# Third mixer: the next sequence's front in 18 pieces and the last sequence's end in 4, each in a slot of its own

## The chip, the cores and the metric

The kernel runs on one core of a Trainium2 chip. The core has a matrix engine (PE, its weight loads shown apart as PEld), a vector engine (DVE), a scalar engine (ACT), a general engine (POOL) and a queue that issues transfers (SP). Each engine works through its own instructions strictly in their order and waits on semaphores for the others. The metric is the device time of one execution in microseconds (us): the median of three runs of the kernel before is 4921.96 us, the runs lie between 4916.99 and 4925.75 us.

## The reference

The model has four layers, each a mixer and a feed-forward part, on 8 sequences of 512 positions by 256 channels in float32. Every part is added to the residual stream X in the same way: `x = x + layernorm(part(layernorm(x)))`. Only the third mixer (called L2 in the code) is touched. Cut to what matters it is causal attention with 16 heads of 16 channels:

```python
q, k, v = silu(x @ Wq.T), silu(x @ Wk.T), silu(x @ Wv.T)   # per head, 16 channels
r_q, r_k = norm(q), norm(k)
scores = (q / (r_q + 1e-6)) @ (k / (r_k + 1e-6)).T * (r_q * q_scale) * (r_k * k_scale)
out = softmax(where(causal, scores, -inf)) @ v
return out @ Wo.T
```

The factor that a head's vector gets, `r / (r + 2e-6 ...)`, needs a square root, which the kernel takes on DVE by a bit trick and three Newton steps (`rsqrt`).

## The kernel before

Everything of a layer for all 8 sequences is written as one Python program. A scheduling layer then orders each engine's queue: instructions that are ready by its own time model go first in the order in which the program wrote them, an instruction whose inputs are late is overtaken, and semaphores are added for every dependence. Buffers come from pools: a pool tile with `bufs=1` cannot be written for the next sequence until its last reader of this sequence is done.

In `l2_attn` (line 1299) the work of one sequence has three parts.

- The **front** (`front`, line 1355, a Python generator; each `yield` ends a piece). `K.late` loads the second layer's feed-forward result (tile `yl`) and adds its normed value to X: `add_norm` takes the statistics of four tiles on DVE (`bn_stats`, `bn_aggr`, then `rsqrt` on 128x4 numbers: tiles `onst`, `onmv`, `onv`, `ony`, `onh`, `onw`, `onb`), scales on ACT (`yn`) and adds on POOL (`X`, two halves). `K.norm` takes the statistics of the new X (`lnst` to `lny`) and writes `xn`, all on DVE. `K.norm_T` turns `xn` on PE (`pxT`) and copies it on ACT (`xT`). Four pieces multiply a block of rows by the weights of q and k (`pqk`), with tanh on ACT (`thqk`), the product on DVE (`qkp`), its square on POOL (`sq`) and the sum over each head on DVE (`ss`). The fifth goes from the sums through `rsqrt` on 128x128 numbers to the factor `f` in one go (tiles `qkny`, `qknh`, `qknw`, `f`), then POOL multiplies `qkp` by `f`; four pieces make v (`pv`, `thv`, `va`).
- The **steps** (the loop at line 1541). Four heads make a quad, a sequence has 4 quads and a quad 4 steps, so a sequence has 16 steps; they are numbered 0 to 15 here. In a step `maxima` makes the scores of four heads for one block of 128 queries (PE: `S`, in two pairs), and DVE takes their masked maxima (`junk`, `mx`). Five steps later `weights` makes the transposed scores (PE: `T`), ACT the exponentials (`PT`) and POOL zeroes the masked corner of the diagonal block; `sums` multiplies by v one step later (PE: `o`). `S` has three PSUM buffers, `T` two: PE can start a score block only when DVE has read the one three before it. `keys` and `strips` turn the next quad's keys and queries (`ptk`, `ptq`) in steps 1 and 2 of a quad; `spread` divides and turns a quad's result back (`pot`, `rs`, `O`).
- The **end** of the last sequence (`finish`, line 1512): it turns O (`pOT`, `OT`), multiplies by Wo (`py`) and calls `add_norm` with the statistics taken straight from PSUM. It is called one step after the last `spread`, in step 8 of the next sequence, as one piece.

A list tells after which steps a piece of the next sequence's front is written; nothing fixes where the scheduling layer then puts it:

```python
PACE = (1, 1, 1, 1, 0, 1, 1, 1, 1, 1, 1, 2, 0, 0, 1, 0)
```

Of the kernel before, what the change touches and what calls it, by code (L numbers as in the profile page):

```python
# [9 lines left out]
F32 = mybir.dt.float32  # L10
I32 = mybir.dt.int32
# [3 lines left out]
ALU = mybir.AluOpType  # L15
# [4 lines left out]
P = 128  # L20
NB = 8
L = 512
NT = 4
D = 256
# [844 lines left out]
def l1_attn(K):  # L869
# [10 lines left out]
    with ExitStack() as es:  # L880
# [12 lines left out]
        nc.gpsimd.tensor_copy(mask[:, L - P:L], K.caus)  # L893
        QT, kT, V, OT = {}, {}, {}, {}
        RATE = (0, 0, 3, 5, 5, 5, 10, 9)
# [55 lines left out]
        def weigh(b, h, PT):  # L951
            po = pO.tile([P, L], F32, tag="o", name=f"o{b}_{h}")
            for kt in range(NT):
                nc.tensor.matmul(
                    po[:, kt * P:L], lhsT=V[b][:, kt, :], rhs=PT[:, kt, kt * P:L],
                    start=(kt == 0), stop=(kt == NT - 1))
            nc.scalar.copy(OT[b][:, h, :], po)

        def finish(b):
            K.project_out(  # L960
                b, [(OT[b][:, h, :], wo[:, h, :]) for h in range(H)], pmm, "mm", s1, leave=True,
                parts=4)

        def behind(b, h, qt, p):

            if qt == 0:
                if h == 0:
                    OT[b] = s1.tile([P, H, L], F32, tag="OT", name=f"OT{b}")
                PT[b, h] = sT.tile([P, NT, L], F32, tag="PT", name=f"PT{b}_{h}")
# [34 lines left out]
class Choice:  # L1004
# [7 lines left out]
    E, NL, K = 48, 10, 128  # L1012
# [286 lines left out]
def l2_attn(K):  # L1299
# [4 lines left out]
    nc, tc = K.nc, K.tc  # L1304
    w = K.W["l2_attn"]
    W = w[:, 0:1536].rearrange("p (k n) -> p k n", k=2)
    row = w[:, 1536:1568]
    wo = w[:, 2048:2560].rearrange("p (k n) -> p k n", k=2)
    with ExitStack() as es:
        def pool(name, bufs, **kw):  # L1310
            return es.enter_context(tc.tile_pool(name="l2" + name, bufs=bufs, **kw))
        cst, sb, s1, s3 = pool("c", 1), pool("a", 2), pool("b", 1), pool("d", 3)
        pmm = pool("pm", 2, space=PSUM)
# [33 lines left out]
        def twice_silu(dst, ps, h, uid):  # L1347

            t = sb.tile([P, 512], F32, tag="th", name="th" + uid)[:, 0:16 * h]
            nc.scalar.activation(t, ps, AF.Tanh, scale=0.5)  # L1350
            return nc.vector.scalar_tensor_tensor(
                dst, t.rearrange("p (h d) -> p h d", h=h), 1.0,
                ps.rearrange("p (h d) -> p h d", h=h), ALU.add, ALU.mult)

        def front(b, res):

            QKP, VA = qkp[b % 2], va[b % 2]
            K.late(b, s1)
            yield
            xn = K.norm(b, s1)  # L1360
            yield
            xT = K.norm_T(b, s1, pmm, "mm", xn=xn)
            yield
            ss = sb.tile([P, NT * 32], F32, tag="ss", name=f"ss{b}")
            for n in range(NT):
                ps = pmm.tile([P, 512], F32, tag="mm", name=f"pqk{b}_{n}")
                for k in range(2):
                    nc.tensor.matmul(
                        ps, lhsT=xT[:, k, n * P:(n + 1) * P], rhs=W[:, k, 0:512],
                        start=(k == 0), stop=(k == 1))  # L1370
                qk = QKP[:, n, :, 0:16]
                twice_silu(qk, ps, 32, f"qk{b}_{n}")
                sq = s1.tile([P, 32, 16], F32, tag="sq", name=f"sq{b}_{n}")
                nc.gpsimd.tensor_tensor(sq, qk, qk, ALU.mult)
                nc.vector.tensor_reduce(ss[:, n * 32:(n + 1) * 32], sq, AX.X, ALU.add)
                yield

            r = K.rsqrt(ss, NT * 32, "qkn", sb)
            nc.vector.tensor_tensor(r, r, ss, ALU.mult)
            f = sb.tile([P, NT, 32], F32, tag="f", name=f"f{b}")  # L1380
            ff = f.rearrange("p n h -> p (n h)")
            nc.vector.tensor_scalar(ff, r, 2e-6, None, ALU.add)
            nc.vector.reciprocal(ff, ff)
            nc.vector.tensor_tensor(ff, ff, r, ALU.mult)
            nc.vector.tensor_tensor(
                f, f, half_row[:, None, :].to_broadcast([P, NT, 32]), ALU.mult)
            yield
            for n in range(NT):
                nc.gpsimd.tensor_tensor(
                    QKP[:, n, :, 0:16], QKP[:, n, :, 0:16],  # L1390
                    f[:, n, :, None].to_broadcast([P, 32, 16]), ALU.mult)
            res.update(QKP=QKP, VA=VA)
            yield
            for n in range(NT):
                pv = pmm.tile([P, D], F32, tag="mm", name=f"pv{b}_{n}")
                for k in range(2):
                    nc.tensor.matmul(
                        pv, lhsT=xT[:, k, n * P:(n + 1) * P], rhs=W[:, k, 512:768],
                        start=(k == 0), stop=(k == 1))
                res["v"] = twice_silu(VA[:, n, :, 0:16], pv, 16, f"v{b}_{n}")  # L1400
                yield
# [10 lines left out]
        def strips(i):  # L1412

            b, g = quads[i]
            ps = turned(res[b]["QKP"], g, f"q{b}_{g}")
            QTs[i] = s3.tile([P, L], F32, tag="QT", name=f"QT{b}_{g}")
            nc.scalar.copy(QTs[i], ps)
# [31 lines left out]
        def lower(i):  # L1449

            b, g = quads[i]
            ps = turned(mx[i % 2], 0, f"m{b}_{g}")
            nc.vector.tensor_tensor(QTs[i], ps, QTs[i], ALU.add)

        def weights(i, kt, js):

            b, g = quads[i]
            KZ, QT = KZs[i], QTs[i]
            n = L - kt * P
            if js[0] == 0:  # L1460
                PTs[i, kt] = s3.tile([P, 4, L], F32, tag="PT", name=f"PT{b}_{g}_{kt}")[:, :, 0:n]
            PT = PTs[i, kt]
            tiles = []
            for j in js:
                ps = pT.tile([P, L], F32, tag="T", name=f"T{b}_{g}_{kt}_{j}")
                half = slice(64 * (j // 2), 64 * (j // 2) + 64)
                nc.tensor.matmul(  # L1467
                    ps[:, 0:n], lhsT=KZ[half, j % 2, kt * P:(kt + 1) * P],
                    rhs=QT[half, kt * P:L], start=True, stop=True)
                tiles.append(ps)  # L1470
            for j, ps in zip(js, tiles):
                nc.scalar.activation(PT[:, j, :], ps[:, 0:n], AF.Exp)  # L1472
            if js[-1] == 3:

                nc.gpsimd.affine_select(  # L1475
                    PT[:, :, 0:P], PT[:, :, 0:P], pattern=[[0, 4], [1, P]],
                    compare_op=ALU.is_ge, fill=0.0, base=0, channel_multiplier=-1)
# [32 lines left out]
                    rs[:, 4 * n:4 * n + 4, :].to_broadcast([P, 4, 16]), ALU.mult)  # L1510

        def finish(b, O):
            OT = s1.tile([P, 2, L], F32, tag="OT", name=f"OT{b}")
            for k in range(2):
                ps = pmm.tile([P, L], F32, tag="mm", name=f"pOT{b}_{k}")
                for n in range(NT):
                    nc.tensor.transpose(
                        ps[:, n * P:(n + 1) * P], O[:, n, k * P:(k + 1) * P], K.ident)
                nc.scalar.copy(OT[:, k, :], ps)
            K.project_out(  # L1520
                b, [(OT[:, k, :], wo[:, k, :]) for k in range(2)], pmm, "mm", s1, leave=True, parts=2)

        res = [{} for _ in range(NB)]
        fronts = [front(b, res[b]) for b in range(NB)]
        quads = [(b, g) for b in range(NB) for g in range(4)]
        QTs, KZs, PTs, pos, OSs, O = {}, {}, {}, {}, {}, {}
        NQ, LAG, KEYS = len(quads), 5, (1, 2, 3, 0)  # L1530
        PACE = (1, 1, 1, 1, 0, 1, 1, 1, 1, 1, 1, 2, 0, 0, 1, 0)

        padding(0)
        for _ in fronts[0]:
# [6 lines left out]
        for s in range(4 * NQ + LAG + 8):  # L1541
            i, qt = s // 4, 3 - s % 4
            k, kt = (s - LAG) // 4, KEYS[(s - LAG) % 4]
            last, lt = (s - LAG - 1) // 4, KEYS[(s - LAG - 1) % 4]
            for js in ((0, 2), (1, 3)):
                if i < NQ:
                    maxima(i, qt, js)
                if js[0] and 0 <= last < NQ:
                    sums(last, lt)
                if 0 <= k < NQ:  # L1550
                    weights(k, kt, js)
            if qt == 0 and i < NQ:
                lower(i)
            if i + 1 < NQ and qt == 2:
                keys(i + 1)
            if i + 1 < NQ and qt == 1:
                strips(i + 1)
            k, r = (s - LAG - 6) // 4, (s - LAG - 6) % 4
            if r == 0 and 0 <= k < NQ:
                b, g = quads[k]  # L1560
                if g == 0:
                    O[b] = s1.tile([P, NT, D], F32, tag="O", name=f"O{b}")
                spread(b, g, OSs.pop(k), O[b])
                QTs.pop(k)
                KZs.pop(k)
            if r == 1 and 0 <= k < NQ and k % 4 == 3:
                finish(k // 4, O.pop(k // 4))
            b = s // 16 + 1
            if b < NB:
                for _ in range(PACE[s % 16]):  # L1570
                    next(fronts[b], None)

# [654 lines left out]
```

## Time and profile before

| what | us |
|---|---|
| median of three runs | 4921.96 |
| profiled execution, its own time | 4924.23 |
| its span, first to last instruction | 4922.5 |
| third mixer, first score block to last transposed score | 2038.0 to 2808.0 |
| sequence 0 of it (first score block to the next sequence's) | 86.9 |
| sequences 1 to 6 | 97.3, 96.5, 96.7, 97.1, 106.0, 96.4 |
| sequence 7, with 6.0 us put for its last step | 78.8 |

In the profile a line such as `L1438 PE MATMUL S<-KZ,QT` names the code line, the engine, the operation and the tiles written and read. A matmul of float32 is two PE instructions. `idle before ... <-X` is time in which the engine had nothing to do, and what ended it. `PEclk` is the share of PE's full clock that was granted in a stretch.

### The profile page before, as it was taken

The page shows a single profiled execution, that of the slowest core. Times are in us where ns is not written, and L with a number is a line of the kernel's source. Part 1 is how long each engine was busy: PE and PEld are TensorE (multiplying, and loading weights), DVE is VectorE, ACT ScalarE, POOL GpSimd, SP SyncE. Part 2 cuts the span into 40 slices and gives each one's busy share as a digit, 9 for nine tenths or more (in the row PEclk, how much of TensorE's full clock was granted, in tenths as well). Part 3 has the DMA queues.
Part 4 walks back from the last instruction along what each step waited for, and adds up shares of the span by engine and source line. Part 5 has one row for each costly group of instructions (what it writes and reads, how often), then busy time and mean ns, then how long its engine had stood idle before and what let it go on. Part 6 is the DMA issues. An engine that isn't in the chain of part 4 may idle for free.

```text
span 4922.5 us, 56985 instructions
## 1 busy us (share of the span) xinstructions
PE 4245.9 (86%) x19078; PEld 2592.8 (53%) x19078; DVE 2890.7 (59%) x8043; ACT 1883.3 (38%) x3801; POOL 1944.0 (39%) x1283
## 2 busy tenths in 40 slices
PE   8745788999988599699999899788888888899997
PEld 3334676555655599355444455333333333478884
DVE  6998746456757411666666433477777777751115
ACT  5410233344344233344443433455555455421112
POOL 0001211444344243333332200398778779613331
PEclk9877798999999799799999999899999999899999
DMA  3289430100000499100000000011111111126763
GB/s 113 79 185 202 127 83 15 43 9 6 6 9 15 125 253 247 29 5 10 5 5 1 22 1 1 28 50 46 41 46 44 43 44 50 64 86 229 232 200 107
DMA packets 401496, 358.04 MB, mean 73 GB/s; under 512 B 209234, under 2 KB 334020, under 8 KB 400692
## 3 DMA queue, kind: packets, MB, share of 16 engines
q1 hardware_dynamic: 373252, 305.75, 21.8%
q0 software_dynamic: 16272, 31.87, 2.4%
q10 hardware_dynamic: 11680, 16.80, 1.1%
q8 instruction: 151, 2.47, 0.2%
q14 instruction: 141, 1.16, 0.1%
HBM read 288.08 MB, written 66.26 MB: 72 GB/s over the span
## 4 chain that ended last, share of the span: by engine, by line
PE 41%; DVE 15%; POOL 4%; ACT 3%; issue 3%; DMA 1%; POOLq 0%; DVEq 0%; SPq 0%; ACTq 0%
DVE h L1777 7%; PE gb L1856 5%; PE S L1438 4%; PE h L1267 4%; PE g L1605 3%; PE T L1467 3%; PE y L1748 3%; PE yb L1870 3%; DVE dB L1723 2%; PE py L193 2%; PE pc L1670 2%; PE y L1278 2%; PE o L1489 2%; POOL h L1780 1%; PE pi L1656 1%
## 5 line engine op out<-in xcount | busy, mean ns | idle before, releaser
L1780 POOL TENSOR_TENSOR h<-h,C 128x1024 f32<-128x1024 f32 x256 | 596.0, 2358 | 177.2 <-DVE h L1777 143.3
L1748 PE MATMUL y<-h,C 128*128 128x512 f32 x1024 | 537.9, 666 | 97.3 <-POOL h L1780 97.3
L1777 DVE TENSOR_TENSOR_SCAN h<-dA,dB 128x512 f32<-128x512 f32 x512 | 588.8, 1202 | 28.5 <-ACT dA L1774 11.7
L1774 ACT ACTIVATE dA<-dl,A 128x512 f32<-128x512 f32 x512 | 352.6, 691 | 411.0 <-DVE h L1777 402.5
L938 POOL TENSOR_SCALAR p<-p,rs 128x128 f32<-128x128 f32 (+3 forms) x256 | 275.9, 1086 | 416.8 <-DVE rs L937 260.2
L1748 PEld LDWEIGHTS y<-h,C 128*128 128x128 f32 x1024 | 204.1, 210 | 408.5 <-issue 224.8
L182 POOL TENSOR_TENSOR X<-X,yn 128x1024 f32<-128x1024 f32 (+2 forms) x104 | 157.0, 1524 | 578.0 <-ACT yn L177 504.9
L1444 DVE CUSTOM_DVE_ANT_0 junk<-S,mask 128x256 f32<-128x256 f32 (+3 forms) x512 | 249.9, 488 | 174.9 <-PE S L1438 139.1
L1438 PE MATMUL S<-KZ,QT 64*128 64x512 f32 (+3 forms) x1024 | 294.2, 473 | 22.2 <-DVE mx L1444 21.3
L1728 POOL TENSOR_TENSOR dB<-du,B 128x2048 f32<-128x2048 f32 x64 | 289.8, 4528 | 0.1
L1472 ACT ACTIVATE PT<-T 128x128 f32<-128x128 f32 (+3 forms) x512 | 199.9, 435 | 224.3 <-PE T L1467 220.8
L1467 PE MATMUL T<-QT,KZ 64*128 64x384 f32 (+3 forms) x1024 | 251.0, 487 | 15.4 <-ACT PT L1472 14.6
L1856 PE MATMUL gb<-xbT,w_b 128*128 128x256 f32 (+1 forms) x1472 | 255.3, 332 | 1.0 <-ACT ts L2060 0.6
L1723 DVE TENSOR_TENSOR dB<-du,pb 128x2048 f32<-128x2048 f32 x64 | 145.4, 2273 | 170.4 <-PE pb L1720 120.7
L1856 PEld LDWEIGHTS gb<-xbT,w_b 128*128 128x128 f32 x1472 | 230.2, 191 | 23.1 <-ACT ts L2060 0.8
L1862 DVE TENSOR_TENSOR hTb<-sb,gb 128x512 f32<-128x512 f32 x71 | 48.8, 687 | 325.4 <-PE gb L1856 314.2
L1475 POOL TENSOR_SCALAR_AFFINE_SELECT PT<-PT 128x512 f32<-128x512 f32 x128 | 81.4, 636 | 330.9 <-ACT PT L1472 330.9
L1438 PEld LDWEIGHTS S<-KZ,QT 64*128 64x128 f32 x1024 | 140.7, 192 | 114.6 <-issue 49.3
L1272 ACT ACTIVATE hT<-h,w_l_ffn 128x128 f32<-128x128 f32 x384 | 109.5, 368 | 198.0 <-PE h L1267 198.0
L1267 PE MATMUL h<-xgT,w 128*128 128x128 f32 x1536 | 185.1, 279 | 0.0
L105 DVE BATCH_NORM_STATS2 lnst<-X 128x6 f32<-128x256 f32 x256 | 99.5, 417 | 135.3 <-POOL X L182 134.4
L1267 PEld LDWEIGHTS h<-xgT,w 128*128 128x128 f32 x1536 | 178.2, 194 | 0.0
(510 smaller groups left out, 9003.9 us busy)
## 6 DMA issues: line engine op xcount, KB each, us to landing
w_b<-l3f_w SPq DMA_DIRECT2D x138, 512.0 KB
w<-l1f_w SPq DMA_DIRECT2D x48, 1024.0 KB
C<-xdd SPq DMA_DIRECT2D x128, 256.0 KB
B<-xdd SPq DMA_DIRECT2D x64, 256.0 KB
w<-l1f_w SPq DMA_DIRECT2D x48, 256.0 KB
toep<-l0fd SPq DMA_DIRECT2D x32, 320.0 KB
X<-x SPq DMA_DIRECT2D x16, 512.0 KB
toep<-l0fd SPq DMA_DIRECT2D x32, 256.0 KB
```

The costliest lines, as they stand in the source:

```text
L938: nc.gpsimd.tensor_scalar(p[:, 0:n], p[:, 0:n], rs, None, ALU.mult)
L1267: nc.tensor.matmul(ph[:, j, :], lhsT=w1[:, s, c, m * P:(m + 1) * P], rhs=xgT[:, c, :], start=(c == 0), stop=(c == 1))
L1438: nc.tensor.matmul(ps[:, 0:n], lhsT=QT[half, qt * P:n], rhs=KZ[half, j % 2, 0:n], start=True, stop=True)
L1444: nc.vector.tensor_tensor_reduce(out=junk[:, 0:n], in0=ps[:, 0:n], in1=mask[:, L - n:L], scale=1.0, scalar=-3.0e38, op0=ALU.add, op1=ALU.m ...
L1467: nc.tensor.matmul(ps[:, 0:n], lhsT=KZ[half, j % 2, kt * P:(kt + 1) * P], rhs=QT[half, kt * P:L], start=True, stop=True)
L1723: nc.vector.tensor_tensor(dB, du, pb[:, None, :].to_broadcast([P, 4, L]), ALU.mult)
L1728: nc.gpsimd.tensor_tensor(dB, du, B[:, None, :].to_broadcast([P, 4, L]), ALU.mult)
L1748: nc.tensor.matmul(py[2 * j + c], lhsT=K.ident, rhs=h[:, c, :], start=False, stop=(n == NS - 1))
L1774: nc.scalar.activation(dA, dl[:, c, :], AF.Exp, scale=A[:, c, n:n + 1])
L1777: nc.vector.tensor_tensor_scan(hs[-1][:, c % 2, :], dA, dB[:, c, :], 0.0, ALU.mult, ALU.add)
L1780: nc.gpsimd.tensor_tensor(h, h, C[:, None, :].to_broadcast([P, 2, L]), ALU.mult)
L1856: nc.tensor.matmul(ps[:, q, :], lhsT=ww[:, k, (c + q) * P:(c + q + 1) * P], rhs=xT[:, k, :], start=(k == 0), stop=(k == 1))
```

## The change

Four things change, all in `l2_attn`.

- `root` replaces the call of `K.rsqrt` in `front`: the same instructions, with a `yield` after the first guess and after each Newton step. A further `yield` follows the reciprocal. The front has 18 pieces in place of 13.
- `finish` becomes a generator of 4 pieces: turning O; the two halves of the product with Wo, each copied by ACT to a new tile `Y` in SBUF; and `add_norm`, whose statistics now read `Y`.
- A table `NEXT` gives each of the 18 pieces a step and a half of the step (after the first pair of heads or at the step's end), and `LAST` gives the 4 pieces of the end theirs.
- `held` opens `issue_after` for the last instruction written so far on PE, DVE, ACT and POOL, so that on each of these engines a piece stands behind that step in the queue. It adds no semaphore and doesn't hold the transfers of SP.

```diff
+        def root(v, n):
+            y, h, w = (sb.tile([P, n], F32, tag="qkn" + c, name="qkn" + c) for c in "yhw")
+            yi = y.bitcast(I32)
+            nc.vector.tensor_single_scalar(yi, v.bitcast(I32), 1, ALU.arith_shift_right)
+            nc.vector.tensor_scalar(yi, yi, -1.0, float(0x5F3759DF), ALU.mult, ALU.add)
+            nc.vector.tensor_scalar(h, v, -0.5, None, ALU.mult)
+            yield
+            for _ in range(3):
+                nc.vector.tensor_tensor(w, h, y, ALU.mult)
+                nc.vector.tensor_tensor(w, w, y, ALU.mult)
+                nc.vector.scalar_tensor_tensor(y, w, 1.5, y, ALU.add, ALU.mult)
+                yield
+            nc.vector.tensor_tensor(y, y, v, ALU.mult)
+            return y
...
-            r = K.rsqrt(ss, NT * 32, "qkn", sb)
-            nc.vector.tensor_tensor(r, r, ss, ALU.mult)
+            r = yield from root(ss, NT * 32)
...
             nc.vector.reciprocal(ff, ff)
+            yield
...
-            K.project_out(
-                b, [(OT[:, k, :], wo[:, k, :]) for k in range(2)], pmm, "mm", s1, leave=True, parts=2)
+            yield
+            Y = s1.tile([P, NT, D], F32, tag="Y", name=f"Y{b}")
+            for half in range(2):
+                ps = pmm.tile([P, 2, D], F32, tag="mm", name=f"py{b}_{half}")
+                for j in range(2):
+                    n = 2 * half + j
+                    for k in range(2):
+                        nc.tensor.matmul(
+                            ps[:, j, :], lhsT=OT[:, k, n * P:(n + 1) * P], rhs=wo[:, k, :],
+                            start=(k == 0), stop=(k == 1))
+                nc.scalar.copy(Y[:, 2 * half:2 * half + 2, :], ps)
+                yield
+            K.add_norm(b, [Y[:, n, :] for n in range(NT)], s1, parts=2)
...
-        PACE = (1, 1, 1, 1, 0, 1, 1, 1, 1, 1, 1, 2, 0, 0, 1, 0)
+        NEXT = {(0, 0): 1, (0, 1): 1, (1, 1): 1, (2, 0): 1, (3, 0): 1, (5, 0): 1, (6, 0): 1,
+                (6, 1): 1, (7, 0): 1, (7, 1): 1, (8, 0): 1, (8, 1): 1, (9, 0): 1, (9, 1): 1,
+                (10, 0): 1, (11, 0): 1, (12, 0): 1, (14, 0): 1}
+        LAST = ((8, 1), (9, 0), (10, 1), (12, 1))
+        ends = {}
...
+        def held(stack):
+            traced, seen = nc.cur_bb.bb.instructions, set()
+            for x in reversed(traced):
+                if x.engine in ENGINES and x.engine not in seen:
+                    seen.add(x.engine)
+                    stack.enter_context(tc.issue_after(x))
+                    if len(seen) == len(ENGINES):
+                        break
+
+        def among(s, half):
+            b, at = s // 16, (s % 16, half)
+            with ExitStack() as stack:
+                held(stack)
+                if b + 1 < NB:
+                    for _ in range(NEXT.get(at, 0)):
+                        next(fronts[b + 1])
+                if b and at in LAST:
+                    next(ends[b - 1], None)
...
                 if 0 <= k < NQ:
                     weights(k, kt, js)
+                if js[0] == 0:
+                    among(s, 0)
...
-            if r == 1 and 0 <= k < NQ and k % 4 == 3:
-                finish(k // 4, O.pop(k // 4))
-            b = s // 16 + 1
-            if b < NB:
-                for _ in range(PACE[s % 16]):
-                    next(fronts[b], None)
+                if g == 3:
+                    ends[b] = finish(b, O.pop(b))
+            among(s, 1)
```

In the queues that result, the work outside this mixer stands in the same order as before, and SP's queue is the same throughout. In the middle sequences the order repeats from sequence to sequence, and these are its points in the changed kernel:

- DVE: `onst` to `onb` of the next sequence stand among the maxima of step 0, `lnst` to `xn` among those of step 1 and wholly ahead of the maxima of step 2; the Newton pieces stand one by one among the maxima of steps 6 to 9; `onst` to `onb` of the last sequence's end stand between the maxima of steps 12 and 13. Before, the fifth piece of the front, the end's `onst` to `onb` and the `onst` to `onb` of the sequence after next all stood among the maxima of steps 8 to 10.
- ACT: the four `yn` stand ahead of the exponentials of step 1, and those of the end between the exponentials of step 13.
- POOL: `X` stands ahead of the corner of step 1; the four products of `qkp` with `f` stand behind the keys of step 9 and ahead of a corner of step 10; the end's `X` stands in step 13.
- PE: `pxT` stands inside step 2, behind its first pair of `S`, with the rest of that step behind it.
- The statistics of the feed-forward part that follows (`lnst` to `lny` of sequences already finished) stood in sequence 5 before and stand in sequence 6 now.

## The prediction

> **What bounds the kernel now.** The change touches one stage, so I read that stage alone, with all of its windows cut where a score block begins (first `S` matmul of a step). A first look goes to whole sequences and to sequence 7, which has no front of a next one. The columns are the busy times of PE, PEld, DVE, ACT and POOL with instruction counts, PE's granted clock, and transfers.
>
> ```profile
> 2318.70:2415.40 96.70, 91.86 (x547) 47.76 (x546) 60.49 (x251) 41.90 (x98) 35.49 (x37) 0.95 0.02 7
> 2512.50:2618.40 105.90, 96.63 (x545) 48.88 (x544) 70.43 (x322) 41.99 (x98) 35.60 (x37) 0.94 0.02 6
> 2714.90:2731.50 16.60, 16.57 (x121) 8.86 (x120) 9.34 (x39) 7.75 (x19) 5.46 (x7) 1.00 0.01 1
> 2731.50:2748.20 16.70, 16.66 (x122) 8.91 (x120) 9.37 (x39) 7.86 (x19) 5.58 (x7) 1.00 0.01 1
> 2748.20:2775.30 27.10, 25.14 (x148) 14.16 (x146) 13.27 (x61) 11.79 (x27) 8.14 (x9) 0.87 0.00 1
> ```
>
> A bare quad takes 16.7 us with PE busy throughout. A sequence in PE's own pace is then 4 x 16.7 = 66.8, plus the pieces by their lengths in the chain of waits: four `pqk` of 1.72, `pxT` 1.2, four `pv` of 0.86, `pOT` 1.1 and `py` 3.5, together 16.1: 82.9 us. It takes 96.7, so 13.8 us are lost in each of six sequences. The quads of sequence 3 show where:
>
> ```profile
> 2318.65:2336.35 17.70, 17.67 (x129) 9.76 (x128) 9.44 (x39) 8.76 (x21) 5.56 (x7) 1.00 0.08 22
> 2336.35:2358.14 21.79, 21.76 (x126) 10.29 (x126) 11.63 (x41) 9.21 (x20) 7.95 (x9) 1.00 0.03 9
> 2358.14:2393.52 35.38, 30.61 (x156) 15.75 (x153) 24.98 (x109) 14.59 (x33) 16.05 (x16) 0.86 0.00 1
> 2393.52:2415.38 21.86, 21.86 (x145) 11.99 (x141) 14.48 (x64) 9.35 (x24) 5.97 (x7) 1.00 0.01 1
> ```
>
> The first two run at PE's pace (16.7 + 1.0, 16.7 + 3 x 1.72). The third should take 16.7 + 1.72 + 4.6 + 0.86 = 23.9 and loses 11.5; the rest is in the fourth. The timelines of DVE and PE in it say why; brackets hold the idle time and what ended it.
>
> ```profile
> 2369.85 0.29 DVE L94 TENSOR_TENSOR qknw<-qknh,qkny 128x128 f32<-128x128 f32 x1
> 2383.21 0.16 DVE L170 SCALAR_TENSOR_TENSOR onb<-onmv,ony 128x4 f32<-128x4 f32 x1
> 2391.00 0.75 DVE L105 BATCH_NORM_STATS2 lnst<-X 128x6 f32<-128x256 f32 x2 [5.55 <-POOL X L182]
> ```
> ```profile
> 2377.23 1.29 PE L1467 MATMUL T<-QT,KZ 64*128 64x384 f32 x4 [1.57 <-ACT PT L1472]
> 2383.77 1.22 PE L1438 MATMUL S<-KZ,QT 64*128 64x256 f32 x2 [1.79 <-DVE mx L1444]
> ```
>
> From 2366 to 2383 DVE does the Newton chain, the end's statistics and those of the sequence after next in one block, with few maxima between; PE runs out of score buffers, and its clock is halved (0.86 in this quad, 0.57 in step 10 alone).
>
> **The change part by part.** No instruction goes; two copies change their place. What moves is which chain meets which step. All prices are of one sequence and are losses against PE's own pace, so none can fall below nothing.
>
> 1. The Newton chain leaves the block: gain. Sequence 7 has the end's chain with no front beside it, in the quad of 27.1 us above: 16.7 + 4.6 = 21.3 at PE's pace, so the end alone loses 5.8. The other 13.8 - 5.8 = 8.0 go with the Newton chain and what stands around it. Split among the maxima of steps 6 to 9 it needs 9 operations of 0.29 us and 2 us more, where DVE is busy 11.6 of 21.8 us (second quad). Left over: 0.5, because step 7 (3.3 us on PE) must hold 1.5 of maxima, 1.6 of `QT`, `rs`, `O` and 1.7 of pieces. Bounds 0 and 1.
>
> 2. The four products on POOL (4.10 us in its timeline) stand behind the keys of step 9 (3.1 us): together 7.8 us after step 10 begins, plus 0.64 for the corner that waits behind them, against 8.0 us until PE asks for it: 0.8, bounds 0 and 2.
>
> 3. The end's chain moves from steps 8-10 to 12-14 and keeps its form: statistics on DVE, `yn` on ACT in front of two exponentials, `X` on POOL. By its queue: maxima of step 12 end 5.1 us into it, `onst` to `onb` takes 4.3 and two maxima of the next step 1.2, so `onb` is there at 10.6, `yn` (2.08) ends at 12.8, and the exponential that PE needs for step 14 at 13.8; PE would be there at 10.9. With the score buffers' wait of 1.5 in step 13 and its clock left full this is 3.2; with one half-clock period 6.4. I take the row of sequence 7, 5.8. Bounds 3.2 and 8.
>
> 4. The chain of the second layer's result moves to steps 0 and 1. Before it lay mostly in the shadow of the block: sequence 6, which has no such chain in its third quad, is no faster (96.5). Now it meets two quads that ran at PE's pace, and PE's queue has `pxT` inside step 2. Counted from the step's start: the first maxima end at 2.7; `onst` x4 1.4, `onmv` 0.4, the small operations at the 0.197 us from one to the next that dependent ones take in the timeline (13 of them), two maxima: `onb` at 8.2. Two `yn` of 0.59 and one half of `X` (1274 ns) put the first `lnst` at 10.7 (two maxima fill 1.4 of the wait), the second pair at 11.9; then aggregates, two maxima, 13 small ones to 16.3, and about 1 more where POOL turns the keys beside them: `xn` from 17.3. PE would be at `pxT` after 4.3 + 5.25 + 0.4 = 10.0. So it stands 7.3 us, broken only by work that waits as well. In the trace stalls such as the two shown were followed by the half clock, in periods of 6.8, 10.2 or 13.7 us; half of the 5 us after 17.3 is 2.6 more. Sum 9.9. Bounds: 7.3 (clock stays) and 12 (another period).
>
> Sum of a middle sequence: 82.9 + 0.5 + 0.8 + 5.8 + 9.9 = 99.9 against 96.6 of the undisturbed ones: +3.3, six times +19.8. The statistics of the next part cost sequence 5 its 9.4 us over the others; they now stand in sequence 6: 0, bounds -5 and +3.
>
> The ends: the prologue loses the second layer's chain of sequence 1, which stood on DVE and POOL ahead of the first keys: -3 (bounds -6, 0). Sequence 0, 86.9: PE's pace 73.1 (5.2 of transposed scores are missing), with 9.9 + 0.5 + 0.8 and 0.7 for a cold start 85.0: -1.9 (bounds -6, +4). Sequence 7: 71.4 + 5.8 + 0.3 = 77.5 against 78.8: -1.3. The tail takes the copy to `Y` ahead of its statistics: +0.7, one copy of 0.59 and its hand-over. SP moves nothing: each `yl` was issued as soon as `xn` was free, a sequence ahead, and still is. Together -5.5.
>
> 19.8 - 5.5 = +14.3. The profiled execution (4924.23, span 4922.5 and 1.7 around it) becomes 4938.5; it stands 2.3 above the median, so 4936.
>
> The Trainium skill, page "TensorE: Matmul & The Clock Gate", section "What's actually happening", states half rate after an idle window of about 3.4 us and full rate after a busy one. By the page alone the short stalls of point 3 keep the clock, the long one of point 4 does not; the estimate would be 4936 - 6 x 2.6 = 4920. The rows above show the half clock after stalls of 1.57 and 1.79 us that fill no such window, and the sum goes by the rows.
>
> **The rivals.**
>
> - *Faster: the pieces hide.* If DVE gets through steps 0 to 2 before PE needs `xn` badly, and the clock stays full, point 4 is 7.3, point 3 3.2 and the others 0.5: 93.9 a sequence, 6 x -2.7 = -16, with -9 at the ends -25: 4897. For it: DVE is busy 60 of 97 us, so there is room over the sequence. Against: PE's queue is strict, and the chain DVE, ACT, POOL, DVE of 15 us has only 10 us of PE work ahead of `pxT`. It decides when `xn` comes within some 15 us of the step's start.
> - *Much slower: two half-clock periods a sequence*, each of two or three windows: 12 + 8 + 3 + 82.9 = 105.9, 6 x 9.3 = +56, -3 at the ends: 4975. For it: the stalls in step 14 and steps 1-2 lie some 13 us apart, and a period took up to 13.7. Against: each before was followed by 75 us or more of full clock in most sequences.
> - *No change*: points 1 and 4 cancel (8.0 - 0.5 - 0.8 = 6.7 gained, about 7.6 lost) and only the ends count: 4915 to 4926.
>
> **How the numbers follow.** What a measurement of this kernel tells from no change is about 0.2%, 10 us. My forecast (98.5 to 102 us a middle sequence) has 0.45, much slower 0.12, no change 0.15, faster 0.28. The range reaches into both outer cases: 4890 to 4972. The forecast's own range is 4928 to 4952. Its lowest part, 0.02, lies within 0.2%. Chances: faster 0.28, same 0.15 + 0.02 = 0.17, slower 0.43 + 0.12 = 0.55.
>
> **What would show it.** Right: in the changed profile the third quads of sequences 1 to 6 fall from 35.4 to 24-26 us, the first rise from 17.7 to 28-32, with `pxT` waiting for DVE `xn` for several us and PE's clock under 1 there; the fourth rise from 21.9 to 23-26 with `T` waiting for ACT behind `yn`. Wrong: first quads under 25 us (DVE's chain shorter than its queue), or third quads over 28 (the Newton chain was not what cost there), or a clock of 1.00 through whole sequences.

## Result: 0.5% slower, and the profile after

The changed kernel takes 4944.86 us (median of five runs, 4942.03 to 4951.74), the kernel before 4919.74 us beside it (five runs, 4916.99 to 4925.75). The ratio is 1.0051 with a 95% interval of 1.0036 to 1.0066. The profiled execution of the changed kernel took 4951.74 us, its span is 4950.0; that is the slowest of its five, 6.9 above its median.

The windows below are of the changed kernel, in the columns of the prediction: sequence 3 whole, sequences 1 to 6 together, then the four quads of sequence 3.

```profile
2333.10:2433.30 100.20, 92.81 (x547) 45.31 (x546) 60.67 (x251) 42.22 (x98) 35.68 (x37) 0.93 0.02 6
...
2128.50:2738.60 610.10, 561.87 (x3265) 275.23 (x3264) 375.21 (x1576) 252.68 (x588) 213.76 (x217) 0.93 0.02 5
...
2333.10:2365.10 32.00, 27.86 (x130) 12.09 (x130) 20.44 (x87) 11.77 (x25) 8.90 (x9) 0.79 0.06 17
2365.10:2388.40 23.30, 22.36 (x140) 10.53 (x138) 13.66 (x53) 9.50 (x23) 9.13 (x10) 1.00 0.00 1
2388.40:2411.60 23.20, 22.94 (x155) 12.99 (x154) 13.02 (x52) 10.62 (x25) 9.61 (x11) 1.00 0.00 1
2411.60:2433.30 21.70, 19.66 (x131) 9.71 (x130) 13.56 (x63) 10.33 (x25) 8.04 (x9) 1.00 0.00 1
```

The quads were 17.7, 21.8, 35.4 and 21.9 us; they are 32.0, 23.3, 23.2 and 21.7. The third quad is repaired: PE stands 0.3 us in it, at full clock. The first is spoilt: PE stands 4.1 us and its clock is 0.79. The same window over sequences 1 to 6 of the kernel before reads:

```profile
2124.90:2714.90 590.00, 557.50 (x3267) 290.88 (x3266) 368.67 (x1529) 249.85 (x584) 210.80 (x215) 0.94 0.02 5
```

So 20.1 us came in: PE stands 48.2 us in place of 32.5 (+15.7), and the same matmuls take 4.4 us more at a lower clock. PE's waits over these six sequences say for whom it stands (us in total, times, longest); first the kernel before, then the changed one:

```profile
PE S L1438 <- DVE mx L1444: 15.7, 13, 2.5
PE T L1467 <- ACT PT L1472: 11.0, 7, 2.2
...
```
```profile
PE S L1454 <- DVE mx L1460: 22.0, 19, 2.1
PE pxT L146 <- DVE xn L133: 16.0, 6, 3.9
PE T L1483 <- ACT PT L1488: 8.1, 6, 1.4
...
```

The wait for `xn` at `pxT` is new, and the waits for maxima are 6.3 us more. The timeline of the first quad of sequence 3, DVE and then PE:

```profile
2341.24 0.16 DVE L170 SCALAR_TENSOR_TENSOR onb<-onmv,ony 128x4 f32<-128x4 f32 x1
2343.92 0.75 DVE L105 BATCH_NORM_STATS2 lnst<-X 128x6 f32<-128x256 f32 x2 [1.32 <-POOL X L182]
2350.29 1.85 DVE L133 TENSOR_SCALAR xn<-X,lnmv,lny 128x256 f32<-128x256 f32 x4
```
```profile
2341.94 1.35 PE L1454 MATMUL S<-KZ,QT 64*128 64x384 f32 x2 [2.05 <-DVE mx L1460]
2351.03 0.41 PE L146 MATMUL pxT<-C,xn 128*128 128x128 f32 x2 [2.10 <-DVE xn L133]
2354.18 3.78 PE L1384 MATMUL pqk<-w_l_attn,xT 128*128 128x512 f32 x4
2361.81 1.98 PE L1384 MATMUL pqk<-w_l_attn,xT 128*128 128x512 f32 x4
```

Two stalls of about 2 us are all that PE stands there. The rest is the clock: one `pqk` takes 3.78 us, the next, after the clock is back, 1.98.

### The profile page after: what moved, and what is told of

The parts are those of the page before. It is cut to its first block, busy times and chain, and to the rows that moved or that the text cites. A ratio compares the mean times of both kernels' runs of the same rounds, so it can differ in the third digit from the quotient of the medians.

```text
span 4950.0 us, 56950 instructions
## 1 busy us (share of the span) xinstructions
PE 4248.6 (86%) x19078; PEld 2574.0 (52%) x19078; DVE 2881.4 (58%) x8043; ACT 1883.8 (38%) x3801; POOL 1947.8 (39%) x1283
## 5 line engine op out<-in xcount | busy, mean ns | idle before, releaser
L1801 PE MATMUL y<-h,C 128*128 128x512 f32 x1024 | 536.5, 665 | 102.7 <-POOL h L1833 102.7
L1454 PE MATMUL S<-KZ,QT 64*128 64x512 f32 (+3 forms) x1024 | 259.6, 492 | 26.4 <-DVE mx L1460 25.5
L1483 PE MATMUL T<-QT,KZ 64*128 64x384 f32 (+3 forms) x1024 | 235.4, 479 | 12.1 <-ACT PT L1488 11.5
L1909 PEld LDWEIGHTS gb<-xbT,w_b 128*128 128x128 f32 x1472 | 230.2, 191 | 23.1 <-ACT ts L2113 0.8
L1454 PEld LDWEIGHTS S<-KZ,QT 64*128 64x128 f32 x1024 | 113.2, 195 | 125.1 <-issue 61.0
L927 PE MATMUL S<-kT,QT 128*128 128x128 f32 (+3 forms) x512 | 175.3, 438 | 1.0 <-DVE nm L932 0.9
```

Source lines behind the costliest of these rows:

```text
L1454: nc.tensor.matmul(ps[:, 0:n], lhsT=QT[half, qt * P:n], rhs=KZ[half, j % 2, 0:n], start=True, stop=True)
L1483: nc.tensor.matmul(ps[:, 0:n], lhsT=KZ[half, j % 2, kt * P:(kt + 1) * P], rhs=QT[half, kt * P:L], start=True, stop=True)
L1801: nc.tensor.matmul(py[2 * j + c], lhsT=K.ident, rhs=h[:, c, :], start=False, stop=(n == NS - 1))
L1909: nc.tensor.matmul(ps[:, q, :], lhsT=ww[:, k, (c + q) * P:(c + q + 1) * P], rhs=xT[:, k, :], start=(k == 0), stop=(k == 1))
```

## The experiments

The table has the median, the ratio to the kernel before, measured beside it, with its interval, the time of sequences 1 to 6 with how long PE is busy and stands in them, and the first quad and the third quad of sequence 3 (all from the windows of the profiled executions).

| kernel | median us | ratio | seq. 1-6 | PE busy | PE stands | quad 1 | quad 3 |
|---|---|---|---|---|---|---|---|
| before | 4919.74 | 1 | 590.0 | 557.5 | 32.5 | 17.7 | 35.4 |
| changed | 4944.86 | 1.0051 (1.0036-1.0066) | 610.1 | 561.9 | 48.2 | 32.0 | 23.2 |
| split_only | 4925.81 | 1.0009 (1.0000-1.0019) | 592.6 | 556.1 | 36.5 | 17.7 | 34.8 |
| root_whole | 4951.48 | 1.0068 (1.0051-1.0085) | 611.3 | 569.3 | 42.0 | 31.9 | 24.4 |
| pxt_later | 4923.93 | 1.0007 (0.9997-1.0016) | 590.2 | 549.5 | 40.7 | 29.0 | 23.6 |
| no_late | 4879.29 | 0.9920 (0.9903-0.9936) | 553.8 | 527.0 | 26.8 | 21.8 | 23.2 |
| norm_later | 4896.69 | 0.9956 (0.9939-0.9974) | 562.1 | 531.7 | 30.4 | 21.4 | 23.6 |
| hold_off | 4885.85 | 0.9932 (0.9916-0.9949) | 563.6 | 537.7 | 25.9 | 20.7 | 24.3 |
| fine | 4864.45 | 0.9887 (0.9871-0.9904) | 539.1 | 528.0 | 11.1 | 24.2 | 23.2 |
| ahead_whole | 4907.58 | 0.9961 (0.9947-0.9975) | 579.8 | 548.4 | 31.4 | 22.9 | 27.5 |
| fine_unheld | 4903.44 | 0.9955 (0.9939-0.9972) | 581.1 | 546.7 | 34.4 | 27.0 | 23.4 |

**split_only: the cut alone, in the kernel before.**

```diff
... (root as in the change)
-            r = K.rsqrt(ss, NT * 32, "qkn", sb)
-            nc.vector.tensor_tensor(r, r, ss, ALU.mult)
+            r = yield from root(ss, NT * 32)
...
             nc.vector.reciprocal(ff, ff)
+            yield
...
-        PACE = (1, 1, 1, 1, 0, 1, 1, 1, 1, 1, 1, 2, 0, 0, 1, 0)
+        PACE = (1, 1, 1, 1, 0, 1, 1, 2, 2, 2, 2, 2, 1, 0, 1, 0)
```

> The kernel before with the factor cut in pieces as in the changed kernel, its list of paces lengthened to (1, 1, 1, 1, 0, 1, 1, 2, 2, 2, 2, 2, 1, 0, 1, 0); nothing is held, the end is as before. In the queue that results the scheduling layer puts the Newton steps of a middle sequence next to each other again. Theory (the cut needs the hold to act): third quads of sequences 1 to 6 stay at 33 to 37 us, time 4912 to 4930. Rival (the cut alone spreads the work): third quads 25 to 29, time 4865 to 4890. Rival (the cut itself costs, by its extra pieces): above 4935.

Measured 4925.81 us, no change that counts, as the theory said; the third quad of sequence 3 is still long:

```profile
2363.90:2398.70 34.80, 29.44 (x151) 14.94 (x150) 24.22 (x108) 14.23 (x32) 15.99 (x16) 0.90 0.00 1
```

Here cutting the Newton chain did nothing as long as the scheduling layer might put the pieces together again. The cut by itself neither gained nor cost.

**root_whole: the cut undone in the changed kernel.**

```diff
-        NEXT = {..., (6, 1): 1, (7, 0): 1, (7, 1): 1, (8, 0): 1, (8, 1): 1, (9, 0): 1, (9, 1): 1, ...}
+        NEXT = {..., (8, 0): 6, (9, 1): 1, ...}
```

> The changed kernel with the six pieces from the first guess to the factor f together in the first half of step 8; all else held where it was. Theory of the prediction (the Newton chain cost 8.0 us of the third quad): as one block of about 6.6 us on DVE, away from the end's statistics, it puts third quads of sequences 1 to 6 from 23.2 to 27-31 us, time 4968 to 4995. Rival (the block before was costly only because three chains stood in it together, the Newton chain alone fits): third quads 23 to 25, time 4940 to 4955.

Measured 4951.48 us, and the third quad of sequence 3:

```profile
2385.20:2409.60 24.40, 23.66 (x153) 13.18 (x152) 15.06 (x58) 10.61 (x25) 9.54 (x11) 1.00 0.00 1
```

The theory of the prediction misses: one Newton chain in one piece costs 1.2 us (24.4 against 23.2), not 4 to 8. The first half of the rival holds: the Newton chain alone fits. What cost 12 us in the third quad before was that it stood in one block with others. It needn't be all three: sequence 6 of the kernel before has no second layer's chain in its third quad, only the Newton chain and the end's (and four short statistics of the part that follows), and that quad is as long as the others:

```profile
2657.91:2694.49 36.58, 31.76 (x164) 17.18 (x160) 23.90 (x88) 13.11 (x31) 13.98 (x15) 0.86 0.00 1
```

No run leaves the end's chain alone with the second layer's there, so which pairs cost is open. Over whole sequences even the 1.2 us mostly vanish: the third quads are 1.2 longer in all six, but the second quads are 0.5 shorter, other quads vary too, and sequences 1 to 6 together differ by 1.2 us (611.3 against 610.1). The medians are 6.6 us apart with intervals that overlap, so no price of the whole kernel follows.

**pxt_later: PE asks for `xn` later.**

```diff
-        NEXT = {(0, 0): 1, (0, 1): 1, (1, 1): 1, (2, 0): 1, (3, 0): 1, (5, 0): 1, (6, 0): 1,
-                (6, 1): 1, (7, 0): 1, (7, 1): 1, (8, 0): 1, (8, 1): 1, (9, 0): 1, (9, 1): 1,
-                (10, 0): 1, (11, 0): 1, (12, 0): 1, (14, 0): 1}
+        NEXT = {(0, 0): 1, (0, 1): 1, (3, 0): 1, (4, 0): 1, (5, 0): 1, (6, 0): 1, (7, 0): 1,
+                (7, 1): 1, (8, 0): 1, (8, 1): 1, (9, 0): 1, (9, 1): 1, (10, 0): 1, (10, 1): 1,
+                (11, 0): 1, (12, 0): 1, (13, 0): 1, (14, 0): 1}
```

> The changed kernel with the turn of xn moved from the end of step 1 to the first half of step 3, and the later pieces one step or half a step behind it (four pqk in steps 4 to 7, Newton in 7 to 9, products on POOL at the end of step 10, v in 11 to 14). Theory (PE's queue stands at pxT because only 10 us of work lie ahead of it): 14.5 us now lie ahead and the statistics still take 17.3, so the stall falls from 7.3 to about 3; first quads of sequences 1 to 6 go from 32.0 to 21-25 us (one pqk less in them), second quads 23 to 26, whole sequences from 101.7 to 92-97, time 4880 to 4920. Rival (holding the pieces behind the steps costs by itself): first quads stay above 29, time 4935 to 4955.

Measured 4923.93 us. Both expectations miss. The first quad is 29.0 us although both of its `pqk` have left it, and PE stands 4.9 us in it where it stood 4.1, so the stall did not go; it changed its name. The window and PE's timeline of the first quad of sequence 3:

```profile
2315.70:2344.70 29.00, 24.11 (x129) 12.11 (x128) 19.52 (x86) 10.90 (x25) 8.34 (x9) 0.76 0.02 5
```
```profile
2324.57 1.64 PE L1454 MATMUL S<-KZ,QT 64*128 64x384 f32 x2 [2.06 <-DVE mx L1460]
...
2335.28 1.22 PE L1454 MATMUL S<-KZ,QT 64*128 64x256 f32 x2 [2.83 <-DVE mx L1460]
...
2341.22 1.16 PE L146 MATMUL pxT<-C,xn 128*128 128x128 f32 x8
```

`pxT` now waits for nothing. In place of 2.10 us there, PE waits 2.83 us for a maximum of step 2. DVE's queue is as strict as PE's: all maxima of step 2 stand behind `xn`, and without them no score buffer comes free. The second layer's chain and the norm, in one run on DVE with waits for POOL in it, hold up PE through the maxima whatever PE has next.

**no_late: without the chain.** The second layer's result of sequences 1 to 7 is left out.

```diff
-            K.late(b, s1)
+            if b == 0:
+                K.late(b, s1)
```

> The changed kernel without the second layer's result of sequences 1 to 7: their load, statistics, yn and addition to X are left out, so those sequences lack it. Theory (the chain from yl to xn is what PE waits for): xn is there about 9 us after the step's start, pxT stands less than 1 us, clock full, first quads 18.5 to 22 us instead of 32.0, whole sequences 88 to 92, time 4855 to 4885. Rival (the hold costs, or pxT itself inside step 2): first quads stay above 26, time above 4910.

Measured 4879.29 us, inside the range of its theory; sequences 1 to 5 take 90.0 to 91.7 us, sequence 6, which has the statistics of the feed-forward part that follows, 98.8. The first quad of sequence 3 has the same 130 PE instructions as in the changed kernel:

```profile
2300.10:2321.93 21.83, 21.20 (x130) 9.95 (x130) 15.18 (x65) 9.64 (x21) 6.17 (x7) 1.00 0.00 1
```

PE is busy 21.20 us at full clock against 27.86 at 0.79. So of the 10.2 us that the chain costs the first quad, 6.7 are the half clock and 3.5 are standing. The hold stays in this kernel; it is not what costs.

**norm_later: the two chains parted.** The places of pxt_later, with the norm in the first half of step 2 and the turn at the end of step 3; the lines show the difference to pxt_later.

```diff
-        NEXT = {(0, 0): 1, (0, 1): 1, (3, 0): 1, ...}
+        NEXT = {(0, 0): 1, (2, 0): 1, (3, 1): 1, ...}
```

> The changed kernel with the later places of the run before it, and the statistics and norm of the next sequence's X moved two steps behind the second layer's chain: norm in the first half of step 2, the turn at the end of step 3. In the queue that results DVE has the maxima of steps 1 and 2 between the two chains. Theory as it stands after the first runs (DVE's queue holds the maxima of steps 1 and 2 behind 8.8 us of statistics and two waits for POOL, so PE runs out of score buffers; pxT is only the second to be late): parted chains cost 3 to 4 us each and wait for nobody, first quads of sequences 1 to 6 go from 28.7 to 23.5-26.5, time 4890 to 4912. Rival (PE waits for xn at pxT): xn comes later than before, first quads stay at 28 or more, time 4918 to 4935.

Measured 4896.69 us, as the theory said, with `xn` 3 us later than in the changed kernel (20.2 us after the step's start against 17.2). DVE's timeline has no wait for POOL any more:

```profile
2318.05 1.40 DVE L105 BATCH_NORM_STATS2 lnst<-X 128x6 f32<-128x256 f32 x4
...
2323.89 1.70 DVE L133 TENSOR_SCALAR xn<-X,lnmv,lny 128x256 f32<-128x256 f32 x4
```

First quads came out at 21.2 to 22.3 us, below the 23.5 to 26.5 expected; the turn of `xn` fell into the second quads (25.6 us, 23.1 in pxt_later).

**hold_off: the change without its hold.**

```diff
         def among(s, half):
             b, at = s // 16, (s % 16, half)
             with ExitStack() as stack:
-                held(stack)
```

> The changed kernel without the hold: pieces are written in the same places, but stand nowhere behind the steps by force. In the queue that results the scheduling layer draws the second layer's chain and the norm of the sequence after next forward into the third and fourth quad of a sequence, next to the end's statistics, and keeps most of the Newton steps among the maxima of steps 6 to 8. Theory (what costs is the place of the second layer's chain that the hold forces): first quads 17.5 to 20 us instead of 32, third and fourth together 48 to 56, whole sequences 89 to 95, time 4875 to 4915. Rival (the places in the program cost, held or not): time 4935 to 4955.

Measured 4885.85 us: 59 us faster than the change as made, and 0.7% faster than before. Left free, the scheduling layer draws the second layer's chain a sequence ahead, into the third and fourth quads, and in the first quad of sequence 3 PE stands for next to nothing (20.7 us, just above the 17.5 to 20 that were expected):

```profile
2302.90:2323.60 20.70, 20.66 (x130) 9.98 (x130) 10.45 (x39) 9.63 (x21) 6.32 (x7) 1.00 0.09 27
```

**fine: every chain cut, the late one a sequence ahead, all held.** `cut_stats` is `stats` with its `rsqrt`, with a yield after each pair of tiles, after the aggregates and after each Newton step; `cut_add` does the same for `add_norm`.

```diff
+        def ahead(b, res):
+            y = K.late_load(b, s1)
+            yield
+            yield from cut_add(b, [y[:, n, :] for n in range(NT)])
+            mv, r = yield from cut_stats([x[:, n, :] for n in range(NT)], "ln")
...
-            K.late(b, s1)
-            yield
-            xn = K.norm(b, s1)
-            yield
-            xT = K.norm_T(b, s1, pmm, "mm", xn=xn)
+            xT = K.norm_T(b, s1, pmm, "mm", xn=res.pop("xn"))
...
-            K.add_norm(b, [Y[:, n, :] for n in range(NT)], s1, parts=2)
+            yield from cut_add(b, [Y[:, n, :] for n in range(NT)])
...
+        NEXT = {(0, 0): 1, (1, 0): 1, (2, 0): 1, (3, 0): 1, (5, 0): 1, (6, 0): 1, (6, 1): 1, (7, 0): 1,
+                (7, 1): 1, (8, 1): 1, (9, 0): 1, (9, 1): 1, (10, 1): 1, (11, 1): 1, (13, 1): 1, (14, 1): 1}
+        AHEAD = {(0, 0): 1, (1, 1): 1, (2, 0): 1, (2, 1): 1, (3, 0): 1, (3, 1): 2, (4, 0): 1, (5, 0): 1,
+                 (9, 0): 1, (9, 1): 1, (10, 0): 1, (13, 0): 1, (13, 1): 2, (14, 0): 1, (15, 0): 1}
+        LAST = {(8, 1): 1, (9, 0): 1, (9, 1): 1, (10, 0): 1, (10, 1): 2, (11, 0): 1, (11, 1): 2,
+                (12, 0): 1, (12, 1): 1}
...
+                if b + 2 < NB:
+                    for _ in range(AHEAD.get(at, 0)):
+                        next(aheads[b + 2])
```

> The changed kernel with the three chains of statistics (second layer's result, norm of X, the end's) cut like the Newton chain, at most six small operations or two tiles to a piece; the second layer's result and xn are made one sequence further ahead (for sequence b+2 in steps 1 to 5 and 9 to 15 of sequence b), the end's pieces stand in steps 8 to 12, yn and its addition in two halves. Held as in the changed kernel. In the queue that results no more than about seven short operations stand between two maxima. Theory (DVE's long runs are the whole loss): every quad within 1.5 us of PE's pace, whole sequences 1 to 5 at 83 to 88 us, clock near 1.00 in most, time 4845 to 4875. Rival (losses come from what DVE, ACT and POOL do beside each other, or from the clock, however the work is spread): sequences stay at 92 or more, time above 4895.

Measured 4864.45 us, 1.1% faster than before and 1.6% faster than the change. Sequences 1 to 4 take 87.8 to 88.1 us. The windows of sequence 3 and of its quads:

```profile
2290.80:2378.60 87.80, 86.55 (x548) 44.42 (x547) 61.13 (x252) 42.23 (x98) 35.72 (x36) 1.00 0.03 7
...
2290.80:2314.95 24.15, 24.12 (x144) 10.95 (x143) 14.70 (x60) 10.72 (x24) 7.67 (x8) 1.00 0.09 23
2314.95:2336.00 21.05, 20.96 (x136) 10.54 (x134) 14.38 (x61) 10.85 (x26) 10.44 (x11) 1.00 0.00 1
2336.00:2359.20 23.20, 22.11 (x149) 12.84 (x148) 17.17 (x72) 10.24 (x24) 9.67 (x11) 1.00 0.01 1
2359.20:2378.60 19.40, 19.37 (x125) 10.10 (x125) 14.88 (x62) 10.42 (x24) 7.94 (x8) 1.00 0.00 1
```

DVE does as much as before (61.1 us a sequence), now spread at 14 to 17 us over each quad, and PE stands 1.2 us in the whole sequence at full clock. What is left is in sequence 5 (98.7 us, where 83 to 88 was expected), which has the statistics of the feed-forward part that follows; nothing was done about those.

**ahead_whole: the places of fine, the chains in one piece.**

```diff
-        AHEAD = {(0, 0): 1, (1, 1): 1, (2, 0): 1, (2, 1): 1, (3, 0): 1, (3, 1): 2, (4, 0): 1, ...}
+        AHEAD = {(0, 0): 1, (2, 0): 6, (4, 0): 2, (13, 0): 6, (14, 0): 2}
-        LAST = {..., (10, 0): 1, (10, 1): 2, (11, 0): 1, (11, 1): 2, (12, 0): 1, (12, 1): 1}
+        LAST = {(8, 1): 1, (9, 0): 1, (9, 1): 1, (10, 0): 6, (12, 0): 2}
```

> The places of the run fine, one sequence ahead, but each of the three chains of statistics in one piece again (second layer's from the first half of step 2, norm of X from that of step 13, the end's from that of step 10), yn and xn in one piece each. It tells the place from the cut. Theory (place and cut both count): a chain in one piece costs 2.6 to 3.1 us, as the parted ones did in steps 1 and 4 of norm_later (8.38 against 5.25, 8.73 against 6.2), so whole sequences 1 to 4 are 93 to 97 us against 87.9, time 4893 to 4918. Rival (the place alone counts, a run of statistics hides once PE does not need its result soon): 87.5 to 90 us, time 4860 to 4880.

Measured 4907.58 us and 95.4 to 95.7 us for sequences 1 to 4, as the theory said, but not with its even price for each chain. The first quad lost next to nothing (22.9 us, with the second layer's statistics in it up to the last Newton step; `onb` comes in the second quad). The end's chain in steps 10 and 11 cost most. The windows of the third and the fourth quad, and PE's longest kind of wait in sequence 3:

```profile
2356.40:2383.90 27.50, 23.92 (x149) 13.99 (x148) 18.28 (x69) 10.23 (x24) 9.95 (x11) 0.92 0.00 1
2383.90:2408.10 24.20, 23.44 (x135) 12.05 (x134) 15.73 (x67) 10.85 (x26) 7.90 (x8) 0.88 0.00 1
```
```profile
PE S L1508 <- DVE mx L1514: 4.4, 3, 3.6
```

One stall of 3.6 us, and PE busy 23.44 us in the fourth quad at a clock of 0.88; at full clock an estimate by these two figures is 20.5 (23.44 less 0.12 x 24.2). The stall isn't the length of the chain alone. Between the two maxima around it three operations on 128x4 numbers take 0.76, 1.10 and 0.67 us where 0.16 or 0.17 is usual, about 2 us in excess, and they do so while POOL multiplies `qkp` by `f` (4.10 us from 2372.83) and then zeroes a corner:

```profile
2375.86 1.10 DVE L1391 TENSOR_SCALAR onh<-onv 128x4 f32<-128x4 f32 x1
```

In fine the same operations meet the same products and are as slow (0.97 and 0.67 us for `onv` and `onh`), but maxima stand between them. No run moves POOL's products away from the chain, so how much of the stall is that neighbour's is not shown.

**fine_unheld: fine without the hold.** The edit is that of hold_off.

> The run fine without the hold. In the queue that results the scheduling layer draws the norm of X forward to stand right behind the second layer's chain in steps 1 and 2, both almost in one run, and two Newton steps together. Theory (the hold is worth what it keeps apart): first quads of sequences 1 to 4 at 26 to 32 us instead of 24.15, whole sequences 90 to 96, time 4878 to 4912. Rival (the hold costs by itself, or does nothing once the pieces are short): whole sequences 88 or less, time 4865 or less.

Measured 4903.44 us; the first quad of sequence 3:

```profile
2313.50:2340.45 26.95, 25.51 (x134) 11.09 (x133) 21.35 (x88) 11.94 (x26) 9.77 (x10) 0.94 0.08 21
```

DVE is busy 21.4 of 27.0 us there: the second layer's chain and the norm are together again. With short pieces in places that suit, the hold is worth 39 us by the medians (4864.45 against 4903.44), or 36 when each is taken against the kernel before measured beside it (4920.74 and 4923.92); with the places of the change it costs 59.

## Why the prediction was right, and by which steps it was not

The direction and the size hold: 4936 was predicted, 4944.9 measured, inside the forecast's own range of 4928 to 4952, and PE does stand at `pxT` for `xn`. The sum of the six middle sequences was +19.8 and is +20.1, but that they agree so well is luck: two errors cancel in it. The five sequences without the statistics of the part that follows take 508.6 us, 101.7 each, against 96.8 before: +4.9 in place of +3.3, 9.7 more over six. And those statistics, whose 9.4 us were only to move, cost nothing where they stand now. The terms one by one:

- **PE's own pace, 82.9 us.** Too low. In fine, where next to nothing waits, PE is busy 86.55 us at full clock; a `pqk` takes 1.98 us and a `pv` 1.13 in the timeline where 1.72 and 0.86 were used, which is 2.1 of the 3.7 us that are missing. The 13.8 us lost before are about 10.1 (96.7 - 86.55). The error doesn't cancel in the difference: the new sequence was added up from the pace (82.9 + 17.0 = 99.9) and set against a measured 96.6. What made up for a part of it are losses that were put too high: 101.7 - 86.6 leaves 15.1 in place of 17.0.
- **Point 1, the Newton chain.** "The other 8.0 go with the Newton chain and what stands around it": it went, the third quads fell to 23.2 us (24 to 26 was said). But root_whole shows that the Newton chain by itself is worth 1.2 there; the gain came from taking it and the end's chain apart. A price for each chain, to be added up, was the wrong form: 1.2 alone and 5.8 alone (by the row of sequence 7) make 7.0, and together they cost 12 to 13.
- **Point 2, POOL's products.** Predicted 0.8 (the working as it stands gives 0.4: 7.8 + 0.64 - 8.0); PE stands 0.26 us in the whole third quad. Within the bounds.
- **Point 3, the end's chain.** 5.8 was taken, from the quad of sequence 7. The quad now has the mechanism as described, at less: in sequence 3 PE waits 1.35 us for an exponential behind `yn` and 0.66 for a maximum, 2.0 in all, and the quad did not grow (21.7 us). In four other sequences a half-clock period falls into step 14, the loss is 3.6 and the quad 23.3. The hand count by the queue (3.2) was the better row, and was put aside for the larger. PE's and ACT's timelines:

```profile
2419.95 0.91 PE L1454 MATMUL S<-KZ,QT 64*128 64x384 f32 x2 [0.66 <-DVE mx L1460]
...
2425.27 1.07 PE L1483 MATMUL T<-QT,KZ 64*128 64x256 f32 x4 [1.35 <-ACT PT L1488]
```
```profile
2422.29 2.08 ACT L177 ACTIVATE yn<-Y,onb,ony 128x256 f32<-128x256 f32 x4 [2.62 <-DVE onb L170]
```

- **Point 4, the second layer's chain.** 9.9 was said. Against the 21.2 us of no_late's PE the first quad loses 10.8. The chain was timed right: `onb`, `lnst` and `xn` were put at 8.2, 10.7 and 17.3 us after the step's start and came at 8.1, 10.8 and 17.2. Its split was wrong: not 7.3 of standing and 2.6 of clock, but 4.1 and 6.7. At half clock PE takes longer to reach `pxT`, so part of the stall is worked away slowly instead of stood out. And `pxT` was named as the place where PE stops; pxt_later shows that it is only one of two, and that with it gone the maxima behind `xn` in DVE's queue stop PE as long.
- **The statistics of the part that follows.** Put at 0, with bounds of -5 and +3, because the 9.4 us that they cost sequence 5 were to be paid in sequence 6. They were not paid: sequence 6 takes 101.5 us, the others 100.2 to 102.7, so the move saved about 9.4 us and lies outside the bounds.

```profile
2637.10:2738.60 101.50, 95.08 (x545) 46.89 (x544) 72.20 (x326) 41.91 (x98) 35.68 (x37) 0.93 0.00 1
```

  DVE does 72.2 us of work there in place of 60.7. In no_late, where PE has no second layer's chain to wait for, the same sequence takes 98.8 us against 91.0 of the others on average. So they cost there too, and in the changed kernel they hide behind the chain: the first quad of sequence 6, with most of them, takes 30.5 us, the others 31.4 to 32.9.
- **The ends, -5.5.** This step missed by most on balance: together the ends are +1.5. Sequence 0 was given the loss of a middle sequence, -1.9 in all, and came out at +4.0. It has no transposed scores to fill the first steps, so PE stands at `pxT` once, for 7.9 us:

```profile
2058.60 2.10 PE L146 MATMUL pxT<-C,xn 128*128 128x128 f32 x8 [7.91 <-DVE xn L133]
```

  The prologue gave -0.4 in place of -3, sequence 7 -1.4 (-1.3 was said), the tail -0.7 (+0.7). The first score block of the eleven kernels starts between 2031.6 and 2039.9 us, so the prologue's 3 us can't be told from run to run by one profile.
- **What stands to no step.** The unchanged code behind the mixer took 5.8 us more in the profiled execution; the prediction put it at nothing. It may not be scatter: from the last transposed score to the span's end the changed kernel, root_whole, pxt_later and norm_later, the four that hold the second layer's chain and the norm in steps 0 to 3, take 2119.1 to 2122.3 us, and the other seven 2111.6 to 2116.3. Why is not known.

Sum against the profiled executions (span 4922.5 to 4950.0, +27.5): prologue -0.4, sequence 0 +4.0, middle +20.1, sequence 7 -1.4, tail -0.7, the rest +5.8, to rounding. Predicted: -3, -1.9, +19.8, -1.3, +0.7, 0.

Of the rivals, the faster one would have needed `xn` within 15 us; it came at 17.2. "Two half-clock periods" came true in kind, most middle sequences have a short one in step 14 (8.3 us in place of 6.75) besides those of the first quad, but PE's busy time grew by 0.7 us a sequence only, since the ones of the third quad went away.

The rule of the Trainium skill that was weighed (page "TensorE: Matmul & The Clock Gate", section "What's actually happening": half rate after an idle window of about 3.4 us) would have made it 4920, the time of no change. In the first quad of sequence 3 the rows were right: the stalls were 2.05 and 2.10 us, none as long as that window, and the half clock took 6.7 us. At point 3, where the two readings had parted, it is mixed: after stalls of 0.66 and 1.35 us the clock stayed at 1.00 in sequence 3 and was halved for a while in four others.

## What to carry to other kernels

A chain that is moved out of one crowd must be followed into the steps where it lands, in every in-order queue: here the blocked work was not only the reader of `xn` but all maxima that stood behind it on DVE. Cut the chains and put the cheap pieces where the engine has slack, make far-off results a whole iteration ahead, and hold the order only then: the same hold cost 59 us with long pieces in poor places and gained 36 to 39 with short pieces in good ones. When a wait vanishes because its reader was moved, but the time stays, look for other work behind the same chain: here it was the maxima. And follow where unchanged work lands: statistics that cost 9.4 us in one sequence cost nothing in another that stood anyway.

## What the runs showed of the hardware that was not expected

- The half clock cost more than the stalls that went with it: 6.7 us against 4.1 in the first quad of the changed kernel. It began in step 1, next to the first stall of 2.05 us (the `S` after it takes 1.35 us for two instructions, 0.91 in the quiet fourth quad).
- The same standing does not always bring it. The fourth quad of sequence 2 of the changed kernel has the waits of that of sequence 3 (0.65 and 1.35 us, there 0.66 and 1.35), but a clock of 0.93 in place of 1.00, and PE is busy 21.3 us in place of 19.7:

```profile
2309.80:2333.10 23.30, 21.26 (x131) 10.04 (x130) 13.71 (x63) 10.32 (x25) 8.11 (x9) 0.93 0.00 1
```

  In norm_later PE stands 3.6 us in the first quad of sequence 3 (21.36 less 17.77 busy) at a clock of 1.00, and 3.45 in that of sequence 4 (22.30 less 18.85) at 0.92. What decides it was not settled; it is only seen that over sequences 1 to 6 fine, whose PE stands 11.1 us, keeps 0.99 and the changed kernel, with 48.2, has 0.93. In between the order is not strict: 32.5 us and 0.94 before, 30.4 and 0.98 in norm_later.
